# Another order of the same steps in a decoder layer on one core

## The chip, the cores and the metric

The kernel runs on one core of a Trainium2 chip. The metric is the time of one execution on the device in microseconds (us); the engines are PE (TensorE matmuls, with PEld for its weight loads), DVE (VectorE), ACT (ScalarE), POOL (GpSimd) and SP (SyncE, which here issues nearly all DMAs).

## The reference

A pre-norm decoder layer in f32 on 128 sequences of 128 tokens with 256 features: self-attention with 16 heads of 16, cross-attention to a context of the same shape under one mask for all sequences, and an FFN with ternary weights, a Gelu and a layer norm over its 1024 hidden features. Cut to what matters:

```python
x = x + attn(layernorm(x), Wq, bq, Wk, bk, Wv, bv, Wo, bo)
x = x + xattn(layernorm(x), ctx, ctx, mask, wq, bq, wk, bk, wv, bv, wo, bo)
x = x + ffn(layernorm(x), W_fc, ln_w, ln_b, W_proj)

def attn(x, ...):                       # xattn: the same, masked scores become 1e-9
    scores = einsum('bhqd,bhkd->bhqk', Q, K) / sqrt(16)
    return einsum('bhqk,bhkd->bhqd', softmax(scores), V) @ Wo.T + bo

def ffn(x, W_fc, ln_w, ln_b, W_proj):
    h = gelu(einsum('btd,hd->bth', x, ternary(W_fc)))
    h = layernorm(h) * ln_w + ln_b
    return einsum('bth,dh->btd', h, ternary(W_proj))
```

## The kernel before

The 128 sequences are worked on in 32 groups of 4 (512 tokens). The work is cut into Python generators, the *streams*; each has a letter, and each `next()` issues one *step*, a handful of instructions up to the next `yield`. The order of all instructions on all engines is the order of these steps, and that is written out by hand: the program walks through `START + ORDER * 28 + END`, one letter for each step. Engines run their own instructions in that order and wait for one another through semaphores; nothing reorders them later. ORDER has 112 letters and is one *round*: it advances each stream by one group, with the streams several groups apart.

The streams, with the steps that are named below:

- **A** (`attention`): for every sequence of a group a row of self-attention (s0 to s3), then of cross-attention (c0 to c3). A row passes through these steps. A:max (`maxima`): scores on PE (L700, for cross rows behind the mask's L689) into the two score tiles, and their maxima over keys on DVE (L711). A:tmx (`transposed_maxima`): the maxima transposed on PE (L728) into the `av` bank, and then for self rows `q_max` on DVE (L733), for cross rows two casts on ACT (L743, L747) and two DVE operations (L745, L749). A:sc (`transposed_scores`): scores again, keys on partitions (L761); for cross rows DVE writes the masked ones over (L771, `copy_predicated`). `weights`: two exps on ACT (L794); for self rows in the same step (A:sc+w), for cross rows a step A:w of its own, whose matmuls (L785) first add the maxima. A:out (`outputs`): the weighted values on PE (L806) into the `av` bank, copied to `raw` by ACT (L809); the last row of a group issues ten DMAs on SP (L390, L396).
- **n** (`prepare_self`), 17 steps for a group: n1 loads x; n2, n3 statistics on DVE, then `rstd` and the normalising on POOL; n4, n5 transposes (L304) and ACT's copies; n6 to n9 queries (L324); n10 to n13 keys; n14 to n17 values (L336) and their copies on DVE.
- **k** (`prepare_keys`), 9 steps: k1 loads the context; k2 to k5 keys of the cross-attention (k4 begins their second half in a new bank); k6 to k9 values.
- **c** (`prepare_cross`), 14 steps: c1 the reciprocal of the sums on DVE, its store and the two loads of `factors`; c2 the product on POOL (L414); c3 to c6 the output projection (L336) and its sum into x on DVE (L418); c7, c8 statistics and normalising; c9, c10 transposes; c11 to c14 queries.
- **f** (`finish`), 36 steps: f1 to f10 as c1 to c10 (f9, f10 split the transposes into two parts); f11 to f14 the first half of the hidden layer, four tiles of matmuls (L443), each with its Gelu on ACT (L450); f15 and f16 its statistics on DVE (L275, L276), f16 also `rstd` on POOL and one half of the normalising (L286); f17 the other half on DVE (L286). f18 to f24 are the same for the second half of the tokens. f25 to f28 transposes (L477), scaled by ACT (L486) and DVE (L488); f29, f30 the second matmul (L501) and its sum into x; f31 to f36 the same for the second half, and the store.
- **w**, **t**: constants and ternary weights, in START alone. **x**, **y**, **z**: the last group's `finish_rows`, in END alone.

In `hidden` the source asks for ACT's function tables itself. L438 stands ahead of the first matmul of f11 and of f18, L452 behind the Gelu of f14 and of f21:

```python
        nc.scalar.preload_act_table(AF.Gelu)                    # L438
...
                nc.scalar.activation(g[:, j, n * 512 : (n + 1) * 512], ph, AF.Gelu)
                if j + n == n_rows:
                    nc.scalar.preload_act_table(AF.Exp)         # L452
```

Three PSUM banks (`ps_mm`) serve all steps but those of A; the score tiles take both of `ps_s`, and `av` and the transposed maxima share one bank.

Of the kernel before, what the change touches and what calls it, by code (L numbers as in the profile page):

```python
# [50 lines left out]


START = (
    "nnnnnnwnwnnnwnnnAnAAnnAwnAAnAnAnAAAAAnnAAknnwAnnnnwnccnkAnnAAnnAnAkAcccckcAAcAnAAkccAccccntAAkAAnkAn"
    "AnAAnAkckAnnAnAcAnAnAnntAnAAAckccAccckkAAknAkAnknAnckcnAcAActAAftkAAAncAcAAntAAAffffAffnAnfnAnnAAnAn"
    "kAffnAAkfcfAffkfAAfknncffAAffffAkkfAnfcAcnfAfAffAAccfAc"
)
ORDER = (
    "ncfAfffAAkkAccAAcfcAnnfAAAccAffAAnnkAAnnAnfAnkAAAfffAfffnAAkcnnAnnAnAfkfkcAffffffAAfffAfffAfccccfffA"
    "fkfkAAAncfAn"  # L60
)
END = (
    "cfAfAffAfAcAcffcAfAAckAAxcAkcfffAAfffAAkfAAAAAkffkAcfAcAfffffAffAffccfffAcckcfckfAffAfAkkAfcAcfAAffc"
    "cAcfcAfAfkAAffAkAkfkAAAAfAfAffffAAxxAffAxAfffAxfffyfAfffffyfxAyffffAfxyxxxzxyfxfffzffyxzzffxxxxyyzxx"
    "yyzzzyzzz"
)


# [837 lines left out]
```

## Time and profile before

| | |
|---|---|
| median of 3 runs | 2737.69 us (2736.14 to 2737.96) |
| span of the profiled execution | 2733.8 us, 3.9 us below the median |
| one round of ORDER | 82.83 us |
| START, 28 rounds, END | about 252, 2319 and 163 us |
| granted TensorE clock | 0.998 |
| ACT table loads | 131 of 1.283 us |

The profile is of one execution. The span runs from its first instruction to its last; a time measured on the device holds a little more. A round is read from the start of the same step in two rounds. A timeline row gives start, duration, engine, line, operation, tiles and count, and in brackets the idle time of the engine before it with what ended that.

### The profile page before, as it was taken

To read this page: it belongs to the slowest core of one execution; us is meant where nothing else is said; L and a number is where in the kernel's file an instruction comes from. 1 tells how busy PE (TensorE), PEld (TensorE's weight loads), DVE (VectorE), ACT (ScalarE), POOL (GpSimd) and SP (SyncE) were. 2 spreads that over 40 slices of the span, in tenths; PEclk is the share of its full clock that TensorE was granted. 3 is DMA by queue.
4 is the path that set the end of the run, shared out by engine and by line. 5 is a ranking of instruction groups with operands and counts; after the bars stand their busy time and mean duration, and the time that the engine had idled before them with its cause. 6 is when DMAs were issued, how large, how long until landed. Compare 5 with 4: busy or idle time off the path is not lost.

```text
span 2733.8 us, 77048 instructions
## 1 busy us (share of the span) xinstructions
PE 2676.2 (98%) x32845; PEld 1917.3 (70%) x32845; DVE 2118.7 (78%) x3916; ACT 1579.2 (58%) x2508; POOL 1337.1 (49%) x1425
## 2 busy tenths in 40 slices
PE   7999999999999999999999999999999999999998
PEld 4567777677777767776777776777777777777666
DVE  5677787777787777887777887777877778877777
ACT  3455666655665655665556666556656556665446
POOL 3344554544554554554445545445545445545443
PEclk9999999999999999999999999999999999999999
DMA  4121111221111221122211112211112211212210
GB/s 118 33 50 42 41 41 50 57 57 34 46 44 50 57 58 28 46 49 51 58 42 41 42 50 57 58 42 42 42 49 58 58 31 44 49 49 50 50 26 16
DMA packets 110093, 130.28 MB, mean 48 GB/s; under 512 B 32312, under 2 KB 69048, under 8 KB 109752
## 3 DMA queue, kind: packets, MB, share of 16 engines
q1 hardware_dynamic: 109464, 125.11, 19.0%
q8 instruction: 259, 4.24, 0.6%
q14 instruction: 82, 0.67, 0.1%
q10 hardware_dynamic: 288, 0.26, 0.0%
HBM read 71.38 MB, written 18.84 MB: 33 GB/s over the span
## 4 chain that ended last, share of the span: by engine, by line
PE 89%; DVE 7%; issue 2%; POOL 1%; ACT 1%; DMA 0%; ACTq 0%; DVEq 0%; SPq 0%; POOLq 0%
PE st L761 10%; PE av L806 9%; PE pq L324 9%; PE s L700 9%; PE ph L443 9%; PE py L501 8%; PE pk L324 8%; PE po L336 8%; PE pv L336 8%; PE pt L304 3%; PE pg L477 2%; PE s L689 2%; PE st L785 2%; DVE mx L711 1%; DVE g L488 1%
## 5 line engine op out<-in xcount | busy, mean ns | idle before, releaser
L711 DVE TENSOR_REDUCE mx<-s 128x8 f32<-128x1024 f32 x512 | 601.3, 1216 | 83.0 <-PE s L700 82.5
L794 ACT ACTIVATE w_t<-st 128x1024 f32<-128x1024 f32 x512 | 496.7, 1022 | 202.5 <-PE st L785 122.3
L281 POOL TENSOR_SCALAR rstd<-agg 128x4 f32<-128x4 f32 (+2 forms) x163 | 39.0, 239 | 965.5 <-DVE agg L276 965.5
L286 POOL TENSOR_SCALAR xn<-x,agg,rstd 128x256 f32<-128x256 f32 x378 | 458.4, 1226 | 9.9
L771 DVE COPY_PREDICATED_SCALAR st<-masked_t,masked_score 128x1024 f32 x256 | 316.1, 1280 | 68.1 <-PE st L761 68.1
L414 POOL TENSOR_TENSOR o_raw<-o_raw,factors 128x256 f32<-128x256 f32 x252 | 181.0, 745 | 382.9 <-DMA factors<-by_head 277.0
L809 ACT COPY raw<-av 128x512 f32<-128x512 f32 x256 | 151.0, 590 | 315.3 <-PE av L806 310.4
L486 ACT ACTIVATE g<-pg,ln_w 128x256 fp32r<-128x256 f32 (+1 forms) x520 | 205.8, 473 | 175.8 <-PE pg L477 163.6
L700 PE MATMUL s<-kt,qt 32*128 32x256 f32 x4096 | 298.8, 402 | 3.2 <-ACT w_t L794 2.2
L501 PE MATMUL py<-w_proj,g 128*128 128x256 f32 x2048 | 279.6, 289 | 1.3 <-DVE g L488 0.8
L806 PE MATMUL av<-w_t,v 128*32 128x128 f32 x8192 | 276.9, 276 | 0.5 <-DVE q_max L733 0.5
L806 PEld LDWEIGHTS av<-w_t,v 128*32 128x32 f32 x8192 | 209.0, 109 | 96.7 <-issue 80.0
L443 PE MATMUL ph<-w_fc,xn 128*128 128x512 f32 x1024 | 259.8, 404 | 4.2 <-ACT g L450 1.6
L501 PEld LDWEIGHTS py<-w_proj,g 128*128 128x128 f32 x2048 | 254.1, 189 | 13.2 <-issue 1.3
L286 POOL TENSOR_SCALAR g<-g,agg,rstd 128x1024 f32<-128x1024 f32 x63 | 241.1, 3828 | 6.6
L488 DVE SCALAR_TENSOR_TENSOR g<-pg,ln_w,g 128x256 fp32r<-128x256 f32 (+1 forms) x520 | 212.6, 469 | 30.3 <-ACT g L486 29.9
L700 PEld LDWEIGHTS s<-kt,qt 32*128 32x128 f32 x4096 | 187.8, 185 | 63.7 <-issue 40.2
L443 PEld LDWEIGHTS ph<-w_fc,xn 128*128 128x128 f32 x1024 | 184.8, 188 | 58.7 <-DVE xn L432 10.0
L761 PEld LDWEIGHTS st<-q_max,kt 32*128 32x128 f32 x4096 | 129.2, 186 | 61.1 <-DVE negm_self L722 42.5
L275 DVE BATCH_NORM_STATS2 stats<-g 128x6 f32<-128x512 f32 x256 | 160.9, 670 | 0.8 <-ACT g L450 0.8
L450 ACT ACTIVATE g<-ph 128x512 f32<-128x512 f32 x256 | 146.5, 599 | 25.3 <-PE ph L443 24.2
L761 PEld LDWEIGHTS st<-qt,kt 32*128 32x128 f32 x4096 | 128.1, 186 | 46.3 <-DVE mx L711 26.4
(130 smaller groups left out, 4612.8 us busy)
## 6 DMA issues: line engine op xcount, KB each, us to landing
o_raw<-raw SPq DMA_DIRECT2D x504, 64.0 KB
factors<-by_head SPq DMA_DIRECT2D x126, 256.0 KB
ctx_t<-in_ctx_t_dram SPq DMA_DIRECT2D x32, 512.0 KB
x<-in_x_dram SPq DMA_DIRECT2D x31, 512.0 KB
out_dram<-x SPq DMA_DIRECT2D x31, 512.0 KB
sums<-raw SPq DMA_DIRECT2D x126, 16.0 KB
by_head<-r SPq DMA_DIRECT2D x63, 32.0 KB
raw_w<-in_w_fc_t_dram SPq DMA_DIRECT2D x1, 1024.0 KB
```

Of the source, the lines that this page charges most:

```text
L286: engine.tensor_scalar(dst[:, j], src[:, j], agg[:, j, 0:1], rstd[:, j : j + 1], ALU.subtract, ALU.mult)
L324: nc.tensor.matmul(out, w[:, c, o * P : (o + 1) * P], src_t[:, c], start=(c == 0), stop=(c == CC - 1))
L336: nc.tensor.matmul(rows[:, j], src_t[:, c, (j0 + j) * P : (j0 + j + 1) * P], w[:, c], start=(c == 0), stop=(c == CC - 1),)
L443: nc.tensor.matmul(ph, xn_parts[i][:, c, (j0 + j - at) * P : (j0 + j - at + 1) * P], w_fc[:, c, n * 512 : (n + 1) * 512], start=((i, c) == ...
L488: nc.vector.scalar_tensor_tensor(parts[1][:, f0 + f, tok], pieces[:, f], scales[f], parts[0][:, f0 + f, tok].bitcast(F32), ALU.mult, ALU.s ...
L501: nc.tensor.matmul(rows[:, j], parts[i][:, f, j * P : (j + 1) * P], w_proj[:, f], start=((i, f) == terms[0]), stop=((i, f) == terms[-1]),)
L700: nc.tensor.matmul(s[r // 2][:, r % 2, 2 * o : 2 * o + 2], qt[strip, o, tok], kt[strip, o, :, tok], start=(stage == "self"), stop=True, sk ...
L711: nc.vector.tensor_reduce(mx[:, 2 * half : 2 * half + 2], s[half], AX.X, ALU.max, negate=True)
L761: nc.tensor.matmul(s[r // 2][:, r % 2, n], kt[strip, n // 2, n % 2, tok], added[strip, n // 2, n % 2] if stage == "self" else qt[strip, n ...
L771: nc.vector.copy_predicated(s[half].rearrange("p r n q -> p (r n) q"), masked_t[:, None, :].to_broadcast([P, 8, P]), masked_score[:, :, No ...
L794: nc.scalar.activation(w_t[:, 2 * half : 2 * half + 2], s[half], AF.Exp)
L806: nc.tensor.matmul(av[32 * r : 32 * r + 32, n], v[:, j, head : head + 32], w_t[:, r, n], start=True, stop=True)
```

## The change

The three strings are replaced. Nothing else in the source changes.

```diff
 START = (
-    "nnnnnnwnwnnnwnnnAnAAnnAwnAAnAnAnAAAAAnnAAknnwAnnnnwnccnkAnnAAnnAnAkAcccckcAAcAnAAkccAccccntAAkAAnkAn"
-    "AnAAnAkckAnnAnAcAnAnAnntAnAAAckccAccckkAAknAkAnknAnckcnAcAActAAftkAAAncAcAAntAAAffffAffnAnfnAnnAAnAn"
-    "kAffnAAkfcfAffkfAAfknncffAAffffAkkfAnfcAcnfAfAffAAccfAc"
+    "nnnnwnnnnnnnnnwAnnAAnknAnnAnAkwAAwnAnAnAAAnnAAwnAnncnnwAnnAAncnAAccAckckAcAknckAAAkccAcccntncAAAtkAA"
+    "nnAAkAnnAnAncnkAncAAAncAnnAncAAAccnAckkcAkkAAncknAAcnkknAAkcAcctAfAtncAAnnAAfAnfAtAAffAkAfnfAfAnnAAn"
+    "nAAffnAffAAfkAcffnfAffknAAfffcfAAfckcAnnfkAfffAAfccAfAc"
 )
 ORDER = (
-    "ncfAfffAAkkAccAAcfcAnnfAAAccAffAAnnkAAnnAnfAnkAAAfffAfffnAAkcnnAnnAnAfkfkcAffffffAAfffAfffAfccccfffA"
-    "fkfkAAAncfAn"
+    "cfAnfAffAAnkkcAccfcAnAAfAccAAAfAnnkfAAkAnAnnfAAAkffnAffffnAnnAcAncnnAAfkfkAffffffffAAfcAfAffcfcckfff"
+    "kAffnAAcAnfA"
 )
 END = (
-    "cfAfAffAfAcAcffcAfAAckAAxcAkcfffAAfffAAkfAAAAAkffkAcfAcAfffffAffAffccfffAcckcfckfAffAfAkkAfcAcfAAffc"
-    "cAcfcAfAfkAAffAkAkfkAAAAfAfAffffAAxxAffAxAfffAxfffyfAfffffyfxAyffffAfxyxxxzxyfxfffzffyxzzffxxxxyyzxx"
-    "yyzzzyzzz"
+    "cffAfAffAAffAcffcAAccAAccAAAffAffAAffAkkAAAkffAAkffcAfffAcfAffffAcfffcccfAkkcffkcAffkkAxAAfcAfffAAcf"
+    "ccAfccAAfAAffAkAkAkkAAAAfffAffffAAxxAffAxfAxfffffAAffffffyAyfxyffffAfxxxxyzyfxxfffzffxfyfxyzzxxxzxyz"
+    "zzxyyyzzz"
 )
```

Each new string has as many of each letter as the one that it replaces (START 255, ORDER 112, END 209 letters), so every stream begins ORDER at the same step as before, and within a stream the steps keep their order. What moves is how the streams interleave. The second half of a round of ORDER, decoded, before:

```
... f17 f18 f19 A:tmx.c3 f20 f21 f22 A:w.c2 f23 c3 c4 c5 c6 f24 f25 f26 A:max.s0 f27 k4 f28 k5 A:out.c2 A:sc.c3 A:tmx.s0 n16 c7 f29 A:w.c3 n17
```

and in the new order, from the same place, behind A:max.c3 and f11 to f16:

```
... f17 f18 A:out.c1 A:sc.c2 f19 c3 A:tmx.c3 f20 A:w.c2 f21 f22 c4 f23 c5 c6 k4 f24 f25 f26 k5 A:max.s0 f27 f28 n16 A:out.c2 A:sc.c3 c7 A:tmx.s0 n17 f29 A:w.c3
```

(Before, A:out.c1 and A:sc.c2 stand ahead of f17.) In the first half of the round A:tmx.s1, s2 and s3 follow at once on A:sc+w of the row before, in place of two or three steps later; f5 moves from ahead of A:w.c0 to behind it, n11 and n12 from behind A:out.c0 to ahead of it; k1 eleven places earlier, c2 eight, k9 seven, n2 ten; n9 comes seven places later, f1 five, n1 three. The rest moves by three places or less, or in step with its neighbours.

## The prediction

> **What bounds the kernel now.** I read the page's busy times first, then the windows, then the timeline of one round, and last the two source lines that load ScalarE's function tables. A "round" is one pass of ORDER; step names are those of the section on the kernel (f21 is step 21 of stream f; A:w.c2 is the `weights` step of cross row 2).
>
> ```profile
> span 2733.8 us, 77048 instructions
> PE 2676.2 (98%) x32845; PEld 1917.3 (70%) x32845; DVE 2118.7 (78%) x3916; ACT 1579.2 (58%) x2508; POOL 1337.1 (49%) x1425
> ```
>
> PE is busy 98% of the span. The windows below cut the span at START's end, at one round (1053.31 to 1136.14) and before END's tail. Columns: length, then busy time of PE, PEld, DVE, ACT, POOL.
>
> ```profile
> 0.00:252.00 252.00, 226.77 (x2681) 151.42 (x2681) 176.40 (x342) 116.35 (x173) 104.79 (x123) 0.99 0.23 59
> 1053.31:1136.14 82.83, 82.47 (x1026) 59.25 (x1025) 65.33 (x120) 49.20 (x78) 41.77 (x44) 1.00 0.20 48
> 2571.00:2733.80 162.80, 140.81 (x1540) 107.53 (x1532) 121.81 (x226) 86.44 (x153) 64.28 (x67) 0.98 0.11 28
> ```
>
> A round is 82.83 us and PE is idle for 0.36 us of it; 28 rounds are 2319 us. PE's order is the same work in any order, so the change can only alter waits and what a switch between kinds of step costs. DVE with 65.3 us looks uncritical on average, but not in one stretch, from the second FFN half to the next round's first scores:
>
> ```profile
> 1111.97 0.60 ACT L450 ACTIVATE g<-ph 128x512 f32<-128x512 f32 x1 [0.32 <-PE ph L443]
> 1112.59 1.28 ACT L452 ACT_TABLE_LOAD   x1
> 1113.88 0.59 ACT L809 COPY raw<-av 128x512 f32<-128x512 f32 x1
> 1114.09 2.48 DVE L771 COPY_PREDICATED_SCALAR st<-masked_t,masked_score 128x1024 f32 x2 [0.36 <-PE st L761]
> 1114.49 1.28 ACT L438 ACT_TABLE_LOAD   x1
> 1115.78 1.09 ACT L450 ACTIVATE g<-ph 128x512 f32<-128x512 f32 x2
> 1116.47 0.81 DVE L286 TENSOR_SCALAR g<-g,agg,rstd 128x1024 f32<-128x1024 f32 x1
> 1117.74 1.09 ACT L450 ACTIVATE g<-ph 128x512 f32<-128x512 f32 x2
> 1118.85 1.28 ACT L452 ACT_TABLE_LOAD   x1
> 1120.14 1.94 ACT L794 ACTIVATE w_t<-st 128x1024 f32<-128x1024 f32 x2
> 1121.14 0.24 POOL L281 TENSOR_SCALAR rstd<-agg 128x2 f32<-128x2 f32 x1 [2.38 <-DVE agg L276]
> 1122.75 1.28 DVE L286 TENSOR_SCALAR g<-g,agg,rstd 128x1024 f32<-128x1024 f32 x1
> 1125.52 2.34 DVE L711 TENSOR_REDUCE mx<-s 128x8 f32<-128x1024 f32 x2
> 1130.36 2.46 DVE L771 COPY_PREDICATED_SCALAR st<-masked_t,masked_score 128x1024 f32 x2
> ```
>
> From 1122.75 DVE runs without a gap of note until 1136.93, and PE's steps there start when DVE lets them: f27 takes 0.96 us where other steps of four transposes take 0.44 to 0.53, A:w.c3 0.54 where A:w.c0 takes 0.33. At 1139.68 A:sc+w.s0 starts 0.01 us after DVE ends the maxima it waits for. So this stretch hangs on DVE, and DVE's run starts when f24 (1122.75) may start. That in turn hangs on the last Gelu of f21, at 1118.83.
>
> The second thing to see is the order on ACT: load of the Gelu table (L438), four Gelus, load of the Exp table (L452), and only then the two exps of L794.
>
> ```profile
> L315 ACT ACT_TABLE_LOAD  x1: 1283/1283/1283, 1.7 to 1.7; - x1
> L438 ACT ACT_TABLE_LOAD  x65: 1283/1283/1283, 190.3 to 2719.5; - x65
> L452 ACT ACT_TABLE_LOAD  x65: 1283/1283/1283, 195.5 to 2721.9; - x65
> ```
>
> The source asks for 65 loads at L438 and 65 at L452 (62 FFN halves of stream f, one each of x, y, z). The one at L315 stands nowhere in the source: that line is a plain copy, ACT's first work. So a load is put in by itself where the table wanted is not in.
>
> **The change, part by part.** *The table.* In the order before, none of the 512 exps (L794) stands between an L438 and its L452, in START, ORDER or END. In the new ORDER it reads f18, A:out.c1, A:sc.c2, f19, c3, A:tmx.c3, f20, **A:w.c2, f21**: the two exps of cross row 2 stand between the Gelus of f20 and f21. That is 28 rounds, and END has one more (A:w.c2 between f11 and f12 of the last f). If a load comes where a table is missing, each costs two: Exp ahead of the exps, Gelu ahead of f21. By L438's row a load takes 1.283 us, and 0.03 us lies around it (Gelu ends 1112.57, load 1112.59, next copy 1113.88). Bounds: 0 us if no load comes, 2 x 1.31 = 2.6 us of ACT if both do. I take 2.6: the L315 row is the nearest.
>
> [...]
>
> *What that does in the stretch.* T counts from f11's start (1107.99 in the trace). Every duration is from the rows of the round shown.
> - ACT: Gelu of f14 ends at 4.58 (as before), Exp table to 5.88. Now f17 and f18 stand ahead of A:out.c1, so the Gelu table follows at once, to 7.18; Gelu of f18 to 7.79, copy `raw` 8.39, Gelu of f19 8.99.
> - DVE: statistics of f15, f16 end at 5.74 as before; POOL's `rstd` (0.24 + 0.73) lets f17's 0.81 us run from 6.97 to 7.78, now ahead of A:sc.c2's masking, which takes 2.48 and ends at 10.15 (8.57 in the trace).
> - PE: f18 3.85, out.c1 4.87, sc.c2 5.88, f19 6.98, c3 7.93, tmx.c3 8.85, f20 8.96 to 9.96. w.c2 waits for the masking until 10.17 and ends at 10.5 (wait 0.2).
> - ACT: of tmx.c3's two casts the second waits for DVE's 0.35 us behind the masking: to 10.72. Gelu of f20 11.22. Exp table 12.52. Exps (1.94) 14.47. Gelu table 15.77. **Gelu of f21 16.38**; in the trace it ends at 10.84.
> - What waits behind it: on PE, k4 takes the PSUM bank that f21 used (banks are taken in the order in which they were freed: so reads f29's wait for DVE at its start, on f28's bank) and stands from 14.1 to 16.4. On DVE, f23's second half of statistics (0.68 + 0.21) ends at 17.3 where the trace has 13.07; POOL's `rstd` (1.05 and 0.1 of hand-over) lets f24 start at 18.5 where the trace has 14.77.
> - DVE's run from f24 to the maxima of A:max.s1 holds the same instructions in both orders: f24 1.28, eight L488 3.3, two pairs of maxima, the masking 2.46, `q_max` 0.86, statistics of x 2.3, copies and adds; in the trace 14.1 us from f24's start to the point at which the maxima can start, and 2.36 more. 18.5 + 14.1 + 2.36 = 34.95; the trace has 31.69. **A:sc+w.s0 is 3.26 us later.**
>
> Behind it PE runs its 51.1 us to the next f11 as before, since DVE and ACT have slack there: it does not catch up.
>
> *The rest of the moves.* PE has no instruction more. A:tmx now follows A:sc+w at once (s1, s2, s3), so it needs the copy of the `av` bank: out, then 1.10 us of scores, and the copy ends 1.06 us after they start, so 0 to 0.1 us each (A:tmx.c1 stands so in the trace: 0.165 us in place of 0.109). A:max.c2 takes 1.62 us in place of 1.44 since it waits for exps; f5 (0.86 us) now lies between the exps and it: -0.17. c11 may wait 0.2 for the copy of k7 behind n2's statistics. SP's queue keeps its order (n1, f36's store, f1, out.s3's ten, k1, c1); k1's 512 KB only leaves earlier, hidden by 5 us and more of PE work. On POOL c2 goes ahead of f10's adds: it waits for `factors` to 1.42 and takes 1.44, the adds 2.9, so POOL is free at 5.8 and f16's `rstd` needs it at 5.83: 0; without that cover, each us late is a us on f17. Sum of these: -0.2, bounds -0.5 to +0.6.
>
> A round: 3.26 - 0.2 = 3.1; 28 x 3.1 = 86 us. END's one case: 2.6, bounds 0 and 2.6. The other moves in START and END: PE idles 25 us in START's window and 22 us in the last; a quarter of either way is 12 us; I take 0. Sum against the span: 2733.8 + 86 + 3 = 2823. The median is 3.9 us above the span, so 2826; I say **2825 us**.
>
> **Rivals.**
> 1. *The loads come, but part is absorbed.* For it: DVE has 0.39 us idle ahead of the maxima, and f24 took 1.28 us there against 0.81 for f17. Against: PE idles only 0.36 us a round. If 1.3 us of the wait reach the end: 2738 + 36 = 2774.
> 2. *No load comes*, because one table holds both functions or the tool puts none. For it: this trace has no exp under the Gelu table to show. Against: 130 loads asked for by hand, and L315. Then f21's Gelu ends at 13.8, f24 starts at 15.9, the maxima end at 32.4: +0.7 - 0.35 (rival 1's slack) = +0.35 a round: 2747.
> 3. *Faster.* PE's waits in the stretch go: f27 0.5, A:tmx.s0 0.2, f29 0.17, A:w.c3 0.2, with A:max.c2 0.17 some 1.2 us a round. It decides where no load comes and f24 starts by 14.8; then 1.0 us x 28 is 28 us: 2710. Against: f21's Gelu stands behind 1.94 us of exps in any case.
> 4. *A load between two kinds of work costs double.* 2 x 1.31 us more a round: 3.1 + 2.6 = 5.7, and 2738 + 28 x 5.7 = 2898. Against: the 0.03 us around L452's load.
>
> **How the numbers follow.** Forecast 0.62, rival 1 0.15, rival 2 0.11, rival 3 0.06, rival 4 0.06. The range for 8 in 10 takes the forecast with its bounds (2.6 to 4.2 us a round) and rival 1: 2772 to 2860. A measurement of this kernel can tell about 0.2%, 5.5 us, from no change. Slower: 0.62 + 0.15 + 0.06 + half of rival 2 = 0.89; within 0.2%: 0.05; faster: 0.06.
>
> **What would show it.** The source lines of the loads: 130 and one before; 58 more, at L794 and L450, if I am right. In a round: a load between f20's Gelu and the exps, another behind them; k4 on PE waiting for ACT's `g`; a round of about 86 us; f24 more than 3 us later after f11. I am wrong if no loads appear, or if they do and A:sc+w.s0 starts less than 2 us later after f11 than the 31.7 of the trace.

## The result and the profile after

| | before | after |
|---|---|---|
| median on the device | 2736.91 us (4 runs, 2735.74 to 2737.96) | 2815.57 us (4 runs, 2814.99 to 2815.89) |
| span of the profiled execution | 2733.8 us | 2813.8 us |
| one round (27, start of f11 to start of f11) | 82.83 us | 85.53 us median, 85.82 us mean |

The ratio is 1.0288, interval 1.0274 to 1.0303. The change makes the kernel 2.9% slower. The page of the changed kernel, its first lines and two groups of instructions (count | busy us, mean ns of one | idle time ahead of them and what ended most of it):

```profile
span 2813.8 us, 77041 instructions
PE 2701.0 (96%) x32845; PEld 1920.5 (68%) x32845; DVE 2118.9 (75%) x3916; ACT 1659.5 (59%) x2566; POOL 1366.6 (49%) x1425
L275 DVE BATCH_NORM_STATS2 stats<-g 128x6 f32<-128x512 f32 x256 | 164.9, 676 | 71.7 <-ACT g L450 71.7
L477 PE MATMUL pg<-ident,g 128*128 128x128 f32 x1024 | 153.9, 282 | 60.7 <-ACT g L450 34.7
```

The counts of PE, DVE and POOL are unchanged. ACT has 58 instructions more, 2566 for 2508, and 80.3 us more busy time. No line of the source is new, so the source does not ask for them. The source lines name the 58 (durations are minimum/median/maximum in ns, then the first and last start in us):

```profile
L794 ACT ACT_TABLE_LOAD  x29: 1283/1283/1283, 294.3 to 2752.0; - x29
L450 ACT ACT_TABLE_LOAD  x29: 1283/1283/1283, 297.6 to 2755.2; - x29
L438 ACT ACT_TABLE_LOAD  x65: 1283/1283/1283, 192.3 to 2795.8; - x65
```

No line of before has a load at the exps (L794) or at the Gelus (L450); the 65 loads that the source asks for at L438 are still there. 58 x 1.283 = 74.4 us of ACT's 80.3. The last groups of the page say who waited for it: DVE's statistics of `g` and PE's transposes of `g`, both for the Gelu.

The timeline of the changed kernel, rows chosen from one round, from behind f14's Gelu to ahead of f27 (f11 starts at 1142.31):

```profile
1146.94 1.28 ACT L452 ACT_TABLE_LOAD   x1
1148.23 1.28 ACT L438 ACT_TABLE_LOAD   x1
1149.79 0.81 DVE L286 TENSOR_SCALAR g<-g,agg,rstd 128x1024 f32<-128x1024 f32 x1 [1.18 <-POOL rstd L282]
1149.86 4.33 POOL L286 TENSOR_SCALAR g<-g,agg,rstd 128x1024 f32<-128x1024 f32 x1
1150.52 2.47 DVE L771 COPY_PREDICATED_SCALAR st<-masked_t,masked_score 128x1024 f32 x2
1153.44 0.61 ACT L450 ACTIVATE g<-ph 128x512 f32<-128x512 f32 x1
1154.06 1.28 ACT L794 ACT_TABLE_LOAD   x1
1155.35 1.94 ACT L794 ACTIVATE w_t<-st 128x1024 f32<-128x1024 f32 x2
1157.31 1.28 ACT L450 ACT_TABLE_LOAD   x1
1158.61 0.60 ACT L450 ACTIVATE g<-ph 128x512 f32<-128x512 f32 x1
1159.22 1.28 ACT L452 ACT_TABLE_LOAD   x1
1159.23 0.69 DVE L275 BATCH_NORM_STATS2 stats<-g 128x6 f32<-128x512 f32 x1 [2.47 <-ACT g L450]
1159.26 0.66 PE L477 MATMUL pg<-ident,g 128*128 128x128 f32 x4 [1.24 <-ACT g L450]
1160.78 0.66 PE L477 MATMUL pg<-ident,g 128*128 128x128 f32 x4 [0.87 <-DVE x L418]
1161.34 0.81 DVE L286 TENSOR_SCALAR g<-g,agg,rstd 128x1024 f32<-128x1024 f32 x1 [0.62 <-POOL rstd L282]
1163.64 2.35 DVE L711 TENSOR_REDUCE mx<-s 128x8 f32<-128x1024 f32 x2
```

Between the Gelu of f20 (1153.44) and that of f21 (1158.61) ACT now runs a load, the two exps of A:w.c2 and another load. DVE stands 2.47 us for f21's Gelu; PE stands 1.24 us ahead of f25 and then 0.87 us ahead of f26. The normalising of f24 (1161.34) starts 19.03 us after f11 here, where the round of before had 14.77.

Medians over the rounds, in us after f11's start, beside the steps of the forecast:

| | before | forecast | measured after |
|---|---|---|---|
| f17 on DVE ends | 9.29 | 7.78 | 8.07 |
| masking of A:sc.c2 ends | 8.58 | 10.15 | 10.46 |
| A:w.c2 starts | 10.02 | 10.17 | 9.98 |
| Gelu of f21 ends | 10.85 | 16.38 | 16.67 |
| f24 starts | 14.77 | 18.5 | 18.8 |
| A:sc+w.s0 starts | 31.70 | 34.95 | 34.13 |
| from there to the next A:max.c3 | 49.69 | 49.5 | 49.91 |

27 rounds at 2.99 us more are 80.7 us. Ahead of the first whole round (START and the start of the first pass) it is 3.3 us more, and behind the last round's A:max.c3 4.05 us less: 80.0 us together, the difference of the spans.

Four of the 27 rounds take 87.5 to 87.8 us, two 86.5 and 86.1, and the others 85.1 to 85.8. The four have something that the prediction doesn't speak of. Windows of the changed kernel, two neighbouring stretches of 3.41 us in one of the four (length, busy time of PE, PEld, DVE, ACT, POOL, then the granted PE clock):

```profile
469.38:472.79 3.41, 1.42 (x9) 1.11 (x10) 1.65 (x4) 3.25 (x6) 1.09 (x3) 1.00 0.00 0
472.79:476.20 3.41, 3.41 (x19) 1.31 (x18) 2.19 (x5) 2.22 (x4) 3.41 (x1) 0.50 0.01 2
```

In the first, PE waits for f21's Gelu. In the second it is busy throughout at half clock. Its score matmuls there, A:max.s0, take 2.09 us in the timeline where the same sixteen take 1.15 us in the round shown above:

```profile
474.09 2.09 PE L700 MATMUL s<-kt,qt 32*128 32x256 f32 x16
1162.22 1.15 PE L700 MATMUL s<-kt,qt 32*128 32x256 f32 x16
```

Such a stretch occurs once in each of the four long rounds and costs about 2.1 us (87.6 for 85.5).

### The profile page after: what moved, and what is told of

Read it like the earlier page. It is cut to its first block, busy times and chain, and to the rows that moved or that the text cites. A ratio compares the mean times of both kernels' runs of the same rounds, so it can differ in the third digit from the quotient of the medians.

```text
span 2813.8 us, 77041 instructions
## 1 busy us (share of the span) xinstructions
PE 2701.0 (96%) x32845; PEld 1920.5 (68%) x32845; DVE 2118.9 (75%) x3916; ACT 1659.5 (59%) x2566; POOL 1366.6 (49%) x1425
## 5 line engine op out<-in xcount | busy, mean ns | idle before, releaser
L794 ACT ACTIVATE w_t<-st 128x1024 f32<-128x1024 f32 x512 | 496.8, 1024 | 200.4 <-PE st L785 119.5
L286 POOL TENSOR_SCALAR xn<-x,agg,rstd 128x256 f32<-128x256 f32 x378 | 459.4, 1228 | 9.9
L414 POOL TENSOR_TENSOR o_raw<-o_raw,factors 128x256 f32<-128x256 f32 x252 | 178.4, 732 | 573.5 <-DMA factors<-by_head 396.5
L286 POOL TENSOR_SCALAR g<-g,agg,rstd 128x1024 f32<-128x1024 f32 x63 | 270.9, 4300 | 6.6
L443 PE MATMUL ph<-w_fc,xn 128*128 128x512 f32 x1024 | 271.3, 407 | 2.4 <-ACT g L450 1.6
L477 PE MATMUL pg<-ident,g 128*128 128x128 f32 x1024 | 153.9, 282 | 60.7 <-ACT g L450 34.7
L477 PEld LDWEIGHTS pg<-ident,g 128*128 128x128 f32 x1024 | 110.9, 141 | 137.2 <-ACT g L450 58.1
L358 ACT ACTIVATE kt<-pk,attn_bkh,parity 128x512 f32<-128x512 f32 x128 | 92.6, 774 | 135.3 <-PE pk L324 135.3
```

The costliest lines, as they stand in the source:

```text
L286: engine.tensor_scalar(dst[:, j], src[:, j], agg[:, j, 0:1], rstd[:, j : j + 1], ALU.subtract, ALU.mult)
L443: nc.tensor.matmul(ph, xn_parts[i][:, c, (j0 + j - at) * P : (j0 + j - at + 1) * P], w_fc[:, c, n * 512 : (n + 1) * 512], start=((i, c) == ...
L477: nc.tensor.transpose(pieces[:, f, j * P : (j + 1) * P], g[:, j, (f0 + f) * P : (f0 + f + 1) * P], ident,)
L794: nc.scalar.activation(w_t[:, 2 * half : 2 * half + 2], s[half], AF.Exp)
```

## The experiments

The theory is the prediction's: the exps of A:w.c2 between two Gelus bring two table loads, and these delay f21's Gelu, f24 and DVE's run. The rivals are that the place of the exps costs the time without any load, that the rest of the new order costs it, and that a load has some other price. Where a run is compared with before, the median of before on the same chip was 2738.4 us.

**Undo one move of the new order.** In the changed kernel A:w.c2 goes from ahead of f21 to behind it, and in END behind f14:

```diff
-    ...ffffffffAAfcAfAffcfcckfff
+    ...ffffffffAAfcAffAfcfcckfff
-    ...AxfAxfffffAA...
+    ...AxfxfffAffAA...
```

> The new order with one letter moved in each round: A:w.c2 goes from between f20 and f21 to behind f21 (in END's last group behind f14). Theory (the two exps between the Gelus cost two table loads, 2.6 us of ACT, and these hold up f21's Gelu and with it DVE's run): the 58 loads are gone, 131 in all, f21's Gelu ends some 12 us after f11's start in place of 16.4, a round is 82.5 to 83.2 us and the time 2728 to 2748 us. Rival (the other moves of the change make it slow): the time stays above 2790 us. Rival (half from the loads, half from f17 standing ahead of the masking): 2770 to 2785 us.

Measured: 2732.39 us (11 runs, 2727.76 to 2740.7), ratio 0.9981 (0.9971 to 0.9992). The loads are 131 again, none at L794 or L450. A round is 82.73 us, f21's Gelu ends at 11.97 and A:sc+w.s0 starts at 31.29. The timeline of this kernel over the same stretch (f11 at 1116.28):

```profile
1124.46 0.61 ACT L450 ACTIVATE g<-ph 128x512 f32<-128x512 f32 x1
1126.90 1.09 ACT L450 ACTIVATE g<-ph 128x512 f32<-128x512 f32 x2
1128.01 1.28 ACT L452 ACT_TABLE_LOAD   x1
1129.31 1.94 ACT L794 ACTIVATE w_t<-st 128x1024 f32<-128x1024 f32 x2
1131.99 0.81 DVE L286 TENSOR_SCALAR g<-g,agg,rstd 128x1024 f32<-128x1024 f32 x1 [0.62 <-POOL rstd L282]
```

The two Gelus stand together again, the one load that the source asks for follows, then the exps. All that the change costs hangs on this one move; with A:w.c2 behind f21 the rest of the new order is some 5 us on the good side (0.19%). This doesn't yet tell the loads from the 1.94 us of exps.

**Keep the place, take the loads away.** The changed kernel with its order untouched, but the two activations of cross row 2 of every group copy where they should exponentiate:

```diff
-    def weights(stage, s, added):
+    def weights(stage, s, added, function=AF.Exp):
...
-            nc.scalar.activation(w_t[:, 2 * half : 2 * half + 2], s[half], AF.Exp)
+            nc.scalar.activation(w_t[:, 2 * half : 2 * half + 2], s[half], function)
...
-                w_t = weights(here[0], s, added_here)
+                w_t = weights(here[0], s, added_here, AF.Copy if here[2] == 2 else AF.Exp)
```

> The new order unchanged, but the two activations of row 2 of every cross-attention are copies in place of exps, so that row's weights are left unexponentiated; place, size and number of activations stay. A copy needs no table of its own, so no load is put in. Theory (the loads are what costs): 131 loads, f21's Gelu still stands behind 1.9 us of activations and ends near 13.8 us after f11, a round is 83.0 to 83.4 us and the time 2740 to 2752 us. Rival (it is the place of the two activations ahead of f21's Gelu, the loads are hidden): the time stays above 2800 us.

Measured: 2735.42 us (10 runs, 2729.69 to 2738.4), ratio 0.9984 (0.9975 to 0.9994). No load is added, f21's Gelu ends at 13.82 and a round is 82.98 us. ACT in one round (f11 at 1108.74), from the Gelu of f20 to that of f21, with the two copies at L794:

```profile
1119.40 0.61 ACT L450 ACTIVATE g<-ph 128x512 f32<-128x512 f32 x1
1119.89 1.95 ACT L794 ACTIVATE w_t<-st 128x1024 f32<-128x1024 f32 x2
1121.70 0.63 ACT L450 ACTIVATE g<-ph 128x512 f32<-128x512 f32 x1
```

The round is just below what was expected (83.0) and the total 5 us below it; START and END, which the expectation did not reckon, gain some 4 us in the run further down that has them alone. The 1.94 us of ACT's work ahead of f21 cost 0.25 us a round (82.98 against 82.73); the two loads cost 2.55 us a round (85.53 against 82.98). The rival "the place alone" is out.

**The one move alone, in the kernel before.**

```diff
-    ...AAfffAfffAfccccfffA
+    ...AAfffAfAfffccccfffA
```

> The order before with one letter of ORDER moved: A:w.c2 goes from behind f22 to between f20 and f21, START and END stay. Theory: 56 table loads more (187 in all). By the rows of the order before, f21's Gelu ends at 15.5 us after f11's start in place of 10.8, f24 starts 2.8 us later, 0.4 us of that is slack ahead of the maxima of A:max.s1: a round of 85.2 us (84.8 to 85.8), time 2804 us (2790 to 2818). Rival (the other moves of the change make it slow): a round stays within 0.3 us of 82.83 and the time below 2747 us.

Measured: 2818.91 us (4 runs, 2814.27 to 2821.74), ratio 1.0294 (1.0277 to 1.031): the whole loss of the change, from one letter moved past two others. Loads: 28 at L794, 28 at L450. f21's Gelu ends at 15.52. The time is 1 us above the range that was expected, and the rounds say why: they alternate, with a few exceptions, between 84.7 and 86, and two are near 87.5. Windows of this kernel, in two neighbouring rounds, the stretch in which PE waits and the one behind it:

```profile
1065.82:1069.23 3.41, 1.37 (x8) 0.70 (x6) 1.16 (x3) 3.36 (x4) 0.17 (x1) 1.00 0.00 0
1069.23:1072.64 3.41, 3.06 (x20) 1.94 (x20) 3.27 (x7) 1.76 (x5) 3.22 (x3) 0.50 0.01 2
1151.15:1154.56 3.41, 1.91 (x10) 1.18 (x8) 0.67 (x1) 3.36 (x4) 0.00 (x0) 1.00 0.00 0
1154.56:1157.97 3.41, 2.54 (x26) 1.81 (x26) 3.35 (x9) 2.46 (x6) 2.87 (x3) 1.00 0.00 0
```

In the first round PE idles 2.04 us (3.41 less 1.37) of one such stretch and the next runs at half clock; in the second it idles 1.50 us and the clock stays full. PE waits 2.37 us in every round (1.50 ahead of f25, 0.87 ahead of f26); what differs is how these two waits fall on a grid of 3.413 us, on which this trace's half-clock stretches begin (1069.23 and 1410.56, 100 x 3.413 apart).

That this total is so near the changed kernel's is in part luck: a round at full clock costs some 1.95 us over before here and 2.70 there, and the half clock adds 0.84 us a round here (the next run but two measures it) and 0.3 there.

**START and END alone.** START and END of the new strings around the ORDER of before.

```diff
 START = (the new one)
 ORDER = (the old one)
 END = (the new one)
```

> START and END of the new order around the ORDER of before. Theory: START and END are worth little; from the traces the new START reaches the first round's A:max.c3 3.3 us later and the new END is 4.0 us shorter, two table loads of the last group's included: 2733 to 2740 us, 133 loads. Rival (START and END carry a part of the loss of 10 us or more): above 2746 us.

Measured: 2734.14 us (11 runs, 2731.87 to 2739.19), ratio 0.9989 (0.998 to 0.9997), rounds of 82.83 us and 133 loads (END's one pair). START and END bring some 4 us of gain; the loss is in ORDER.

**Two loads without any move.** In the kernel before, with A:w.c2 where it was, an Exp load and a Gelu load ahead of f21's Gelu:

```diff
+                if j0 == 2 and n_rows == 2 and j + n == 2:
+                    nc.scalar.preload_act_table(AF.Exp)
+                    nc.scalar.preload_act_table(AF.Gelu)
                 nc.scalar.activation(g[:, j, n * 512 : (n + 1) * 512], ph, AF.Gelu)
```

> The order before, with two table loads more in the second hidden half of each group of stream f (Exp, then Gelu, ahead of f21's Gelu); A:w.c2 stays behind f22. This is the loads alone, without the exps between them. By the rows of the order before: f21's Gelu ends at 13.5 us after f11 in place of 10.85, f24 starts 0.9 us later, 0.4 us of that is slack; A:max.s0 waits for exps that end at 16.8. Theory (loads and exps both stand ahead of f21's Gelu and only what goes beyond some 3 us of delay reaches PE): a round of 83.3 us (82.9 to 84.3), time 2752 us (2742 to 2780), 62 loads more. Rival (each us of table load costs a us of time, wherever it stands): a round of 85.4 us, 2810 us.

Measured: 2794.81 us (4 runs, 2792.84 to 2797.27), ratio 1.0203 (1.0187 to 1.0218), a round of 84.82 us. The expectation missed: 83.3 us a round was expected, and the rival's 85.4 was nearer. f21's Gelu ends at 13.56 as expected and f24 ends only 0.46 us later than in before. The time comes by another way, in the timeline of this kernel (f11 at 1131.45; its source lines from L450 on are 3 higher, so L453 is the Gelu, L797 the exps, L703 the scores, L480 the transposes):

```profile
1143.11 1.28 ACT L452 ACT_TABLE_LOAD   x1
1144.40 0.60 ACT L453 ACTIVATE g<-ph 128x512 f32<-128x512 f32 x1
1145.02 1.28 ACT L455 ACT_TABLE_LOAD   x1
1146.31 1.94 ACT L797 ACTIVATE w_t<-st 128x1024 f32<-128x1024 f32 x2
1147.39 0.70 PE L703 MATMUL s<-kt,qt 32*128 32x256 f32 x4 [0.16 <-ACT w_t L797]
1148.30 1.13 PE L703 MATMUL s<-kt,qt 32*128 32x256 f32 x12 [0.21 <-ACT w_t L797]
1149.37 0.66 PE L480 MATMUL pg<-ident,g 128*128 128x128 f32 x4
```

The exps stand behind the delayed Gelu here, end at 16.8 us after f11 (14.10 before), and hold the score tiles that A:max.s0 writes to: its matmuls wait twice for `w_t`. f27 follows at 17.92 in place of 16.04, and A:sc+w.s0 is 1.99 us later. The expectation had the 16.8 in it, but reckoned on with DVE's run alone. So the same loads reach PE by another way when the exps stand behind them. Which of the two stands first hardly matters in this order: 84.82 us a round here, 84.7 to 84.8 in the short rounds of the run with the one move, where the exps run first.

In the new order the loads cost more, 2.55 us a round. The rows of DVE say why. With the one move in before, f24 starts 2.88 us later (17.66 for 14.78), but on the way to A:sc+w.s0 two instructions become shorter: f24 itself (0.81 us for 1.26) and the two copies of the maxima of A:max.s0, L722 (0.61 for 1.06). That leaves 1.98; A:sc+w.s0 comes 1.97 later in the rounds at full clock. In the new order both are short without the loads as well (0.81 and 0.60 in the run with the copies), so there is nothing to win back. What ran beside them where they are long is in the last section.

**Fill PE's wait.** The kernel with the one move alone, and in f24 fourteen transposes of the identity into an `av` tile that nothing reads:

```diff
+        if j0 == 2 and n_rows == 2:
+            idle = ps_av.tile([P, 4, P], F32, name="idle", tag="av")
+            for i in range(14):
+                nc.tensor.transpose(idle[:, i % 4], ident, ident)
```

> As b_wc2_early (the order before with A:w.c2 between f20 and f21), with 14 transposes of the identity more on PE in step f24, into the av bank, read by nothing: 1.5 us of PE work where PE stands idle for 1.5 us ahead of f25. Theory (PE's clock is halved for 3.41 us where its idle time, 2.37 us in a round, falls into one stretch of a 3.41 us grid; this makes every other round 86 us in place of 84.8): no halved stretch within the rounds, all rounds at 84.7 to 84.9 us, time 2794 us (2788 to 2802) against 2819. Rival (the halving has nothing to do with the idle time, or the alternation comes from DMA): halved stretches and rounds of 86 us stay, 2815 to 2822 us; or the added matmuls delay PE, above 2822 us.

Measured: 2799.44 us (4 runs, 2798.26 to 2800.14), ratio to before 1.0222 (1.0208 to 1.0236), 19.5 us faster than the kernel without the fourteen. All rounds but one (85.0) are 84.7 to 84.8, and no stretch in them is at half clock. A whole round in the windows, first one of the long rounds without the fourteen, then one with them:

```profile
1052.49:1138.35 85.86, 83.47 (x1028) 59.70 (x1025) 65.07 (x120) 51.95 (x81) 42.37 (x44) 0.98 0.20 46
```

```profile
1047.53:1132.27 84.74, 83.88 (x1042) 60.54 (x1039) 64.28 (x120) 51.96 (x81) 41.80 (x44) 1.00 0.19 46
```

PE does fourteen matmuls more and the round is 1.12 us shorter than the long one, with the clock at 1.00 in place of 0.98. ACT's loads and DVE's run are the same. So in these two kernels the half clock went with PE's idle time, and cost 0.84 us a round in the mean (85.63 against 84.78); the round that is left, 84.78, is what loads and place cost in this order at full clock, 1.95 us over before.

**The parts that gain.** With A:w.c2 behind f21, some stretches of the new ORDER are shorter than in before, some longer. This kernel takes the longer ones back from before: the start of the round (behind A:sc+w.s0 up to A:max.s3), the places of c2 and k3, and f17, f18 behind A:sc.c2. START is the new one, END that of the first experiment.

```diff
-    "cfAnfAffAAnkkcAccfcAnAAfAccAAAfA...AncnnAAfkfkAffffffffAAfcAfAffcfcckfff"
+    "cfAnfAffAkkAccAAcfcAnnfAAccAAAfA...AnnAnAfkfkcAffffffAAfffcAffAfcfcckfff"
```

> a_wc2_late with two stretches of ORDER taken from the order before: from behind A:sc+w.s0 to A:max.s3 (11.74 us in the trace of before, 11.95 in the new order) and from behind n13 to f19 (c2 again behind k3, f17 and f18 again behind A:sc.c2; 0.15 us less). Theory (what is left between the orders is a few tenths of a us a stretch, and the stretches add): a round of 82.4 us, time 2723 us (2716 to 2731), no load more than before. Rival (the stretches hang together through DVE's run): a round of 82.7 us or more, 2730 us and above.

Measured: 2723.36 us (5 runs, 2720.93 to 2727.66), ratio 0.9947 (0.9935 to 0.996) to before: faster than both kernels. A round is 82.38 us, as expected, and A:sc+w.s0 starts at 30.98 (31.70 in before). PE is busy 82.15 of these 82.38 us:

```profile
1104.05:1186.43 82.38, 82.15 (x1029) 59.23 (x1025) 65.41 (x120) 49.44 (x79) 42.34 (x44) 1.00 0.20 49
```

It wasn't tried which of the stretches brings how much.

## Why the prediction was right, and where it was off

The forecast was 2825 us (2772 to 2860), slower with 0.89; the time is 2815.57. By its steps:

- *The loads.* Forecast 58 more, at L794 and L450, 1.283 us each with next to nothing around them. So it is, to the count. Rival 2 (no load) falls with it; the run with the copies gives its price, 82.98 us a round where rival 2 had 83.18. A load starts 0.01 to 0.02 us behind the activation ahead of it and the next activation as soon behind the load (Gelu 1153.44 + 0.61, load 1154.06; load 1157.31 + 1.28, Gelu 1158.61). The median round is 2.70 us longer, where two loads are 2.57 us and rival 4 had 5.7. Rival 4 with its 2898 us falls by these rows.
- *f21's Gelu, f24.* 16.38 forecast, 16.67 measured; 18.5 forecast, 18.8 measured. Both 0.3 us late, and so are f17 and the masking ahead of them (8.07 for 7.78, 10.46 for 10.15). f17 waits for POOL's `rstd`, but that is late because DVE's statistics are: those of f15 and f16 end at 6.04 where the prediction kept 5.74, "as before". Of the 0.3 us, 0.11 are a later end of the maxima of A:max.c3, and 0.19 a small DVE instruction between them and the statistics, L717. First the round of before that the forecast was read from, then that of the changed kernel:

```profile
1109.41 1.44 POOL L414 TENSOR_TENSOR o_raw<-o_raw,factors 128x256 f32<-128x256 f32 x2 [1.88 <-DMA factors<-by_head]
1110.49 0.41 DVE L717 TENSOR_SCALAR negm_cross<-mx,least 128x48 f32<-128x48 f32 x1
1143.60 2.84 POOL L424 TENSOR_TENSOR x<-x,b_proj 128x256 f32<-128x256 f32 x4
1144.92 0.87 DVE L717 TENSOR_SCALAR negm_cross<-mx,least 128x48 f32<-128x48 f32 x1
```

In most rounds of before POOL stands idle at that time and L717 takes 0.25 us. In the new order c2 stands earlier, so that POOL's products and adds run there in 26 of the 27 rounds; L717 then ends 0.04 to 0.08 us behind one of them and takes 0.60 us in the median. In the four rounds in which it takes 0.25 or 0.27 and POOL is free in time for f16's `rstd`, f17 ends at 7.67 to 7.70 and f24 starts at 18.41 to 18.43, within 0.1 us of the forecast.
- *Which step waits.* Wrong: the prediction let k4 stand on PE from 14.1 to 16.4 for the bank of f21. k4 starts at 14.46 with no wait, and f25 stands for ACT's Gelu, then f26 for DVE's sum into x (0.87). The order in which banks come round was misread; the wait's end is the same, and so the sum wasn't hurt.
- *DVE's run.* Forecast +3.26 us at A:sc+w.s0, measured +2.43: the largest miss. The run has no gap left, as forecast, but is 1.1 us shorter than the same instructions in before: f24 takes 0.81 us in place of 1.28, the two copies of the maxima of A:max.s0 (L722) 0.60 in place of 1.06, the rest is small. 0.3 us of later start takes part of that back. That is rival 1 in small, with its own hint (0.81 for f17) as the larger half of the cause; L722 the prediction did not name.
- *The rest of the moves.* Forecast -0.2 us a round within -0.5 to +0.6, measured +0.22. A:max.c2 is back to 1.44 us (-0.17) as forecast. A:tmx.s1 takes 0.195 us (0.109 before), A:tmx.s2 and s3 0.084 (0.202 before). POOL's "each us late is a us on f17" came true in the fourth and the seventeenth round: its adds ended at 7.12 and 6.80 where 5.8 was reckoned, f16's `rstd` at 7.33 and 7.02 in place of some 6.4, and these rounds take 86.5 and 86.1.
- *The clock.* Not foreseen by any term: four rounds of 2.1 us more, 0.3 us a round in the mean. By luck it fills part of the gap that DVE's run left: 2.43 + 0.22 make 2.65 where the median round has 2.70 and the mean 2.99, against 3.1.
- *START and END.* Forecast +2.6 in all; measured +3.3 ahead and -4.05 behind, -0.75 together, within the 12 us either way that were left for them.
- *The sum.* Its own terms make 2827.5 (2733.8 + 28 x 3.1 + 3 + 3.9); 2826 and 2825 are rounded down, which brings the forecast 2 us nearer.
- *Rival 3 (faster)* named its condition, no loads, and f24 by 14.8. The run with A:w.c2 behind f21 has no added loads and f24 at 15.7 (1131.99 less 1116.28); A:sc+w.s0 comes 0.41 us earlier than in before (31.29 for 31.70), and 0.3 us of that is lost in the rest of the round. In the last kernel, with f24 at 15.65, it comes 0.72 earlier and the round is 0.45 shorter. So about half of the 1.0 us that it named is there, under a milder condition than it set.

## What to carry to other kernels

When steps are reordered, write down the order of functions on ACT as the new order gives it, not the order of steps: one step of exps between two Gelus brought two table loads (1.283 us each) that no line of the source asks for, and the explicit loads around it didn't prevent it. Then ask what stands behind the delayed activation; here 2.6 us on an engine that is busy 58% of the time became 2.55 us of every round, since the busiest engine's inputs came from it. And here, with PE busy nearly all the time, a wait had a second price: in the kernel with the single move, where PE's two waits came to 2.04 us of idle time in one stretch of 3.41 us, its granted clock in the next was 0.50; where they fell into two stretches, with 1.50 and 0.87 us, it stayed at 1.00. The half clock cost 0.84 us a round there in the mean.

## What the runs showed of the hardware

*PE's clock.* In the changed kernel all half-clock stretches begin on one grid of 3.413 us: those in its rounds at 472.79, 646.87, 1588.95 and 2104.36, 51, 276 and 151 times 3.413 us apart, each 3.41 us long. Cutting the trace's rounds into the cells of that grid and adding up PE's idle time in each: the four cells ahead of these had 1.91 to 2.10 us of idle at full clock, and none of the cells with less (up to 1.76 us, at 384.04) was followed by half clock. The idle time was not in one piece: ahead of 472.79 PE waited 1.24 us and then 0.86. Full clock followed on each of the four, in which PE had no idle time. The kernel with the single move has its half-clock stretches on such a grid too (1069.23 and 1410.56, 100 x 3.413 apart). There full clock followed on a half-clock stretch with 0.35 us of idle (3.41 less 3.06, at 1069.23), and half clock once more on one with 0.48 us, the second row here; this is one of the two rounds near 87.5:

```profile
1407.15:1410.56 3.41, 1.53 (x9) 0.83 (x7) 1.03 (x3) 3.36 (x4) 0.03 (x1) 1.00 0.00 0
1410.56:1413.97 3.41, 2.93 (x20) 1.94 (x20) 3.39 (x7) 1.89 (x5) 3.22 (x3) 0.50 0.00 0
1413.97:1417.39 3.42, 3.42 (x14) 2.15 (x11) 3.17 (x6) 0.84 (x2) 3.42 (x4) 0.50 0.00 0
1417.39:1420.80 3.41, 3.41 (x70) 2.33 (x69) 1.81 (x6) 2.76 (x5) 1.37 (x2) 1.00 0.02 5
```

These numbers hold for these rounds alone: outside them cells with less idle time were followed by half clock too (1.48 us at 2584 in before, 0.98 us at 29 in the changed kernel). So idle time is not all that counts; what else does wasn't tried.

*DVE and POOL on the two halves of one normalising.* Where POOL starts its half 1.5 us ahead (1.38 to 1.67 over the rounds of before), DVE's takes 0.81 us and POOL's 3.79; where POOL is 0.45 us ahead, DVE's takes 1.28 and POOL's 3.79; where DVE is 0.07 us ahead, 0.81 and 4.33. The first is the f17 of before in the round shown, the second its f24, the third the f24 of after; the difference, 0.47 us, is a good part of the 1.1 us that the forecast of DVE's run had too much. What makes it wasn't tried.

*Small DVE instructions beside POOL's products and adds.* In 26 of the 27 rounds of the changed kernel L717 (0.25 us with POOL idle) ends 0.04 to 0.08 us behind a POOL instruction with two input tiles, L414 or L424, and takes up to 0.87 us. A copy of L722 takes 0.16 us at its shortest. In before both copies of L722 for A:max.s0 end 0.03 us behind an add of POOL, one add apart, in all 27 rounds, which makes 1.06 us of them. In the changed kernel the first ends 0.03 us behind an add and the second, in most rounds, 0.10 us behind the same add: 0.60 us. Beside POOL's normalising (L286, one input tile) it goes either way: in before, L717 takes its 0.25 us in the middle of one in 28 cases and ends 0.26 us ahead of it, while copies of L722 that begin in its last 0.2 to 0.3 us end 0.03 or 0.04 us behind it. What decides wasn't tried.
